# An encoder-decoder layer on one core: five small moves between ScalarE, VectorE and GpSimd

## The chip, the cores and the metric

The kernel runs on one core of a Trainium2 chip. A core has a matrix engine (TensorE, PE in the profile, its weight loads PEld), a vector engine (VectorE, DVE), a scalar engine (ScalarE, ACT), GpSimd (POOL) and SyncE (SP), which issues all transfers of this kernel. Each engine takes its own instructions in order; semaphores order the engines against one another. Results of TensorE go to PSUM, which has eight banks, and are read from there by VectorE or ScalarE.

The metric is the time of one execution on the device in microseconds (us). Before the change three runs took 3012.80, 3021.18 and 3019.86 us; the median is 3019.86.

## What is computed

One encoder layer on a short text (2 batches, 77 rows of width 512) and one decoder layer on a long sequence (2 batches, 2048 rows), all in fp32. 16 heads of width 32, an inner width of 2048. Cut to what matters:

```python
# encoder on ctx (77 rows): attention with relative bias, then relu feed-forward -> memory
yn = _ln(y, dec_n1_s, dec_n1_b)
y = y + _mha(yn, yn, dec_sa_in_w, ..., sb)        # causal self attention, 2048 x 2048, relative bias
y = y + _mha(_ln(y, dec_n2_s, dec_n2_b), memory, dec_ca_in_w, ..., cb)   # cross attention, 77 keys
h = _ln(y, dec_n3_s, dec_n3_b)
y = y + (relu(h @ dec_ff1_w.T + dec_ff1_b) @ dec_ff2_w.T + dec_ff2_b)

# _mha: scores = q k^T / sqrt(32) + bias; softmax over the keys; times v; out projection
# _ln:  (x - mean) * rsqrt(var + 1e-6) * s + b
```

The relative bias is the same for all keys further back than 127, so only the last two tiles of 128 keys of a row tile have a bias of their own.

## The kernel before, in words

The order of all instructions is written out by hand; nothing is scheduled by a tool.

**Self attention** takes up the time to about 1860 us. The sequence is cut into blocks of 512 rows (m = 0 to 3 per batch b) and these into 4 row tiles of 128 (t). Heads go in 4 groups of 4 (g). A unit is one (b, m, g, t): 128 rows against the keys up to and with their own tile, m*4 + t + 1 tiles of 128. These are cut into pieces of up to 4 tiles (`pieces`), and pieces go in pairs.

- `scores` (L344 on): for a piece, four matmuls, one for each head, on 32 rows of TensorE each, into four PSUM banks. In fp32 each is issued as two passes. VectorE then takes each bank to SBUF with its row maximum (L370), or, for the last two tiles, adds the bias (L377) and makes the negated maximum (L384). The exp is ScalarE's (L387); for m of 1 and more it is kept back and issued later by `exps`.
- `turn` (L397 on): for a pair of pieces, TensorE transposes the probabilities, 128 x 128 at a time (L411), up to four into one bank, which makes a load. A load is copied to SBUF by VectorE (L415) or by ScalarE (L417). Line 414 decides which. For m of 1 and more a load is one tile of keys for the four heads; a pair of two full pieces has 8 loads.
- `values` (L422 on): the turned pieces times v (L428), into a bank of their own.

Banks are given out in turn by `bank()`, 7 of them in self attention, so an eighth request waits for the release of the first. The main loop at the end of the kernel goes through the pairs: turn the pair; if the unit ends with it, run the jobs of the next slot (projections for later blocks, out projections, norms, and at first stages of the encoder); then scores of later pieces as far as memory allows, exps between them; then values of the pair.

**First cross attention.** In slots of the second batch's first blocks (about 966 to 1320 us) `first_cross` does the cross attention of the very first block.

**Cross attention and feed-forward**, from about 1862 us. For each of the 8 blocks (x) the feed-forward goes in 56 slots: 28 for the first product, 28 for the second, each by Strassen's scheme with seven products (`PARTS`, taken in the orders `ORDER`) in four quarters. `prepare` makes operands that are sums three slots ahead: on GpSimd, or on VectorE for `h` (L1114). `first_product` (L1125 on) adds a product into one or two quarters of hT; where it is the first to write a quarter it copies instead (L1142 or L1144, ScalarE), else VectorE adds (L1146); after the last, ScalarE adds the bias and takes the relu (L1149). The bank ring has four banks for products and four for all else.

Beside these slots runs the cross attention of the next block (`cross`, a plan with a list of stages for each slot, issued ahead of the slot's product). `norm_stages` has three stages: statistics (L726 to L729), centering on VectorE and the row of biases added on GpSimd (L735, L736), and the turned tile (transposes L741, then scale and bias by four activations, L744). For the norm before the cross attention these run at slots t, t + 2 and t + 4. `attend_stages` for row tile t starts at slot 14 + 7t: scores (L765, VectorE L772 to L775), exp (L778) two slots later, `normalize` three slots later (sums L783, reciprocals L784, product L785), `turned` at 6 (transposes L791, copies L793 and L795), times v at 9 (L802, L806), out projection at 11 (L811, L812). For the first block of a batch the tiles t of 0 and 1 need a bias, loaded by four DMAs into the tile of probabilities before the scores (`bias`, L103).

The lines that decide where things run, before:

```python
if o % 2 if first else o < 3 * len(loads) // 8:      # L414, turn: VectorE's loads
nc.scalar.activation(dst[:, c, :], pt[:, ts(c, P)], AF.Identity, bias=bi, scale=sc)   # L744
(engine or nc.gpsimd).tensor_tensor(prh, prh, ri[:, :, None].to_broadcast([P, H, S]), ALU.mult)  # L785
nc.scalar.copy(dst, got)                             # L1144
plan[at - 1 if t else at - 4].append(lambda t=t: bias(t))
```

Of the kernel before, what the change touches and what calls it, by code (L numbers as in the profile page):

```python
# [11 lines left out]
AF = mybir.ActivationFunctionType  # L12
ALU = mybir.AluOpType
# [4 lines left out]
P = 128  # L18
B, T, S, D = 2, 2048, 77, 512
H, HD, DFF = 16, 32, 2048  # L20
# [34 lines left out]
def tile_encoder_decoder(ctx: ExitStack, tc: tile.TileContext, ins, out):  # L55
    nc = tc.nc
# [92 lines left out]
    with (  # L149
# [245 lines left out]
        got = {}  # L395

        def turn(pieces):  # L397

            first = units[pieces[0][0]][1] == 0
            loads = []  # L400
            for n, k0, kn in pieces:
                ks = range(k0, k0 + kn)
                if first:
                    loads += [[(n, k, r) for k in ks] for r in range(HC)]
                else:
                    loads += [[(n, k, r) for r in range(HC)] for k in ks]
            for o, load in enumerate(loads):
                pt = bank()
                pts = in_turn("pts", pts_all).rearrange("p (x q) -> p x q", q=P)
                for x, (n, k, r) in enumerate(load):  # L410
                    nc.tensor.transpose(pt[:, ts(x, P)], state[n]["p"][r][:, ts(k, P)], ident)  # L411
                    got[n, k, r] = pts[:, x, :]
                w = len(load) * P
                if o % 2 if first else o < 3 * len(loads) // 8:  # L414
                    nc.vector.tensor_copy(pts[:, : len(load), :], pt[:, :w])  # L415
                else:
                    nc.scalar.copy(pts[:, : len(load), :], pt[:, :w])  # L417
                if first and o == len(loads) - 1:
                    exps(1)
            exps(1)  # L420
# [297 lines left out]
        def norm_stages(y, n, row, place, done):  # L718

            keep = {}  # L720

            def stats():
                st = sm.tile([P, 6], F32, name="bnst", tag="bnst")
                mv = sm.tile([P, 2], F32, name="cmv", tag="cmv", bufs=4)
                rs = sm.tile([P, 2], F32, name="crs", tag="crs", bufs=4)
                nc.vector.bn_stats(st, y())  # L726
                nc.vector.bn_aggr(mv, st)
                nc.vector.tensor_scalar_add(rs[:, 0:1], mv[:, 1:2], EPS)
                nc.gpsimd.tensor_tensor(rs[:, 1:2], rs[:, 0:1], mhalf[:, 0:1], ALU.pow)  # L729
                keep.update(mv=mv, rs=rs)  # L730

            def center():
                xn = keep["xn"] = place()
                mv, rs = keep["mv"], keep["rs"]
                nc.vector.tensor_scalar(xn, y(), mv[:, 0:1], rs[:, 1:2], ALU.subtract, ALU.mult)  # L735
                nc.gpsimd.tensor_tensor(y(), y(), row, ALU.add)  # L736

            def turned():
                xn, pt, dst = keep["xn"], bank(), done()
                for c in range(NC):  # L740
                    nc.tensor.transpose(pt[:, ts(c, P)], xn[:, ts(c, P)], ident)  # L741
                for c in range(NC):
                    sc, bi = vec(f"dec_{n}_s", c), vec(f"dec_{n}_b", c)
                    nc.scalar.activation(dst[:, c, :], pt[:, ts(c, P)], AF.Identity, bias=bi, scale=sc)  # L744

            return stats, center, turned

# [3 lines left out]
                nc.tensor.matmul(mm, w[:, c, :], nT[:, c, :], start=(c == 0), stop=(c == NC - 1))  # L751
            nc.vector.tensor_scalar(dst, mm, vec("dec_ca_in_b", o), SCALE, ALU.add, ALU.mult)

        def attend_stages(q, kTc, v, y, biased, pr, pts, place, w_o, engine=None):

            prh = pr.rearrange("p (h k) -> p h k", k=S)
            by_r = pr.rearrange("p (g r k) -> p g r k", r=HC, k=S)
            keep = {}

            def score():  # L760
                mx = sm.tile([P, NC, HC], F32, name="cmx", tag="cmx", bufs=3)
                banks = [bank() for _ in range(HC)]
                for g in range(NC):
                    for r in range(HC):
                        nc.tensor.matmul(  # L765
                            banks[r][:, ts(g, S)], q(g)[rows4(r)], kTc[rows4(r), g, :], start=True, stop=True
                        )
                for r in range(HC):
                    s = banks[r][:, : NC * S].rearrange("p (g k) -> p g k", k=S)
                    d = by_r[:, :, r, :]  # L770
                    if biased:
                        nc.vector.tensor_tensor(d, s, d, ALU.add)  # L772
                        s = d
                    nc.vector.tensor_reduce(mx[:, :, r], s, AX.X, ALU.max)
                    nc.vector.tensor_tensor(d, s, mx[:, :, r, None].to_broadcast([P, NC, S]), ALU.subtract)  # L775

            def exp():
                nc.scalar.activation(pr, pr, AF.Exp)  # L778

            def normalize():  # L780
                su = sm.tile([P, H], F32, name="csu", tag="csu", bufs=2)
                ri = sm.tile([P, H], F32, name="cri", tag="cri", bufs=2)
                nc.vector.tensor_reduce(su, prh, AX.X, ALU.add)  # L783
                nc.vector.reciprocal(ri, su)  # L784
                (engine or nc.gpsimd).tensor_tensor(prh, prh, ri[:, :, None].to_broadcast([P, H, S]), ALU.mult)  # L785

            def turned():
                for g in range(NC):
                    pt = bank()
                    for r in range(HC):  # L790
                        nc.tensor.transpose(pt[:S, ts(r, P)], prh[:, g * HC + r, :], ident)  # L791
                    if g % 2:
                        nc.vector.tensor_copy(pts(g), pt[:S, :])  # L793
                    else:
                        nc.scalar.copy(pts(g), pt[:S, :])  # L795

            def times_v():
                ot = bank()
                for g in range(NC):
                    for r in range(HC):  # L800
                        h = g * HC + r
                        nc.tensor.matmul(  # L802
                            ot[rows4(r), ts(g, P)], v[:, ts(h, HD)], pts(g)[:, ts(r, P)], start=True, stop=True
                        )
                keep["oT"] = place()
                nc.scalar.copy(keep["oT"], ot)  # L806

            def out():
                mm, oT = bank(), keep["oT"]
                for c in range(NC):  # L810
                    nc.tensor.matmul(mm, oT[:, ts(c, P)], w_o[:, c, :], start=(c == 0), stop=(c == NC - 1))  # L811
                nc.vector.tensor_tensor(y(), mm, y(), ALU.add)  # L812

            return score, exp, normalize, turned, times_v, out
# [78 lines left out]
        for x, (b, m) in enumerate(blocks):  # L893
            u = x * NU
            first = m == 0
# [24 lines left out]
            for g in range(NC):  # L920
# [3 lines left out]
                at = u + g * TB - 3  # L924
# [200 lines left out]
        def first_product(s):  # L1125
            x, layer, i, n = slots[s]
            a, b = operands[s]
            mm = ff_bank()
            for f in range(2):
                for c in range(2):  # L1130
                    nc.tensor.matmul(  # L1131
                        mm[:, ts(f, TOK)], a[:, c, ts(f, P)], b[:, c, :], start=(c == 0), stop=(c == 1)
                    )
            order = order_of(x, 1)
            got = mm.rearrange("p (f n) -> p f n", f=2)
            for sign, r, c in PARTS[i][2]:
                users = [j for j in order if (r, c) in [u[1:] for u in PARTS[j][2]]]
                f = (r - 1) * (NF // 2) + 2 * n
                dst = hT[:, f : f + 2, ts(c - 1, TOK)]
                if i == users[0]:  # L1140
                    if sign == "-":
                        nc.scalar.activation(dst, got, AF.Identity, scale=-1.0)  # L1142
                    else:
                        nc.scalar.copy(dst, got)  # L1144
                else:
                    nc.vector.tensor_tensor(dst, dst, got, SIGN[sign])  # L1146
                if i == users[-1]:
                    for e in range(2):
                        nc.scalar.activation(dst[:, e, :], dst[:, e, :], AF.Relu, bias=vec("dec_ff1_b", f + e))  # L1149
# [41 lines left out]
        def cross(x):  # L1191
# [9 lines left out]
            def bias(t):  # L1201
                bias_tile(pr.rearrange("p (h k) -> p h k", k=S), 2, P, S, 255 - P * t)
# [9 lines left out]
            for t in range(TB):  # L1212
                at = 14 + 7 * t
                y = lambda t=t: y_of(x, t)
                biased = m == 0 and t < 2
                if biased:
                    plan[at - 1 if t else at - 4].append(lambda t=t: bias(t))
                fs = attend_stages(
                    lambda g, t=t: qT[g // 2][:, g % 2, ts(t, P)], kTcs[b], vcs[b], y, biased, pr,
                    lambda g: pts_all[:S, g, :], place("xr"), wbt,  # L1220
                    None if t else nc.vector,
                )
                for k, f in zip((0, 2, 3, 6, 9, 11), fs):
                    plan[at + k].append(f)
# [133 lines left out]
```

## Time and profile before

| what | value |
|---|---|
| median of three runs | 3019.86 us |
| profiled execution, its own time | 3012.80 us |
| its span | 3011.0 us |
| TensorE busy | 2952.2 us, 98% of the span |
| VectorE busy | 2032.6 us, 68% |
| ScalarE busy | 1381.3 us, 46% |
| GpSimd busy | 733.6 us, 24% |
| mean TensorE clock granted | 0.99 |

The profile is one execution. The profiled execution's own time is its span and 1.8 us around it. Busy time of TensorE is that of pipelined matmuls, so 98% does not say that it runs at its peak; the chain of work that ended last and the waits tell where it is held. A group's row gives its line, engine, operation, tiles (out<-in) and shape, the count, then the busy time and the mean length of one in ns, then the idle time of the engine just ahead of it and what ended most of that. A row of the list of waits gives total us, number of waits and the longest. In the timeline a line is one instruction, or several of the same kind in a row, with start and length in us. An instruction's length has a tail that the next one on its engine overlaps: VectorE's copy of 128 x 512 from PSUM is 0.68 us long, but three in a row take 1.88 us.

### The profile page before, as it was taken

The page shows a single profiled execution, that of the slowest core. Times are in us where ns is not written, and L with a number is a line of the kernel's source. Part 1 is how long each engine was busy: PE and PEld are TensorE (multiplying, and loading weights), DVE is VectorE, ACT ScalarE, POOL GpSimd, SP SyncE. Part 2 cuts the span into 40 slices and gives each one's busy share as a digit, 9 for nine tenths or more (in the row PEclk, how much of TensorE's full clock was granted, in tenths as well). Part 3 has the DMA queues.
Part 4 walks back from the last instruction along what each step waited for, and adds up shares of the span by engine and source line. Part 5 has one row for each costly group of instructions (what it writes and reads, how often), then busy time and mean ns, then how long its engine had stood idle before and what let it go on. Part 6 is the DMA issues. An engine that isn't in the chain of part 4 may idle for free.

```text
span 3011.0 us, 60727 instructions
## 1 busy us (share of the span) xinstructions
PE 2952.2 (98%) x24440; PEld 2095.8 (70%) x24440; DVE 2032.6 (68%) x5806; ACT 1381.3 (46%) x2583; POOL 733.6 (24%) x594
## 2 busy tenths in 40 slices
PE   8899999999999999999999999999999999999999
PEld 5567666666677556666666677787878687878788
DVE  4766567767886777767867776666666666565645
ACT  3344456656666455556656666323232323232321
POOL 0100000000000101000000002464646464646465
PEclk9899999999999999999999999999999999999999
DMA  6413301200012411201200013200001000000000
GB/s 175 95 48 113 93 15 47 64 19 26 33 40 72 112 47 54 78 26 47 65 19 17 29 61 101 102 29 1 29 1 37 9 29 1 29 1 29 1 15 15
DMA packets 117645, 137.11 MB, mean 46 GB/s; under 512 B 18241, under 2 KB 73073, under 8 KB 117235
## 3 DMA queue, kind: packets, MB, share of 16 engines
q1 hardware_dynamic: 117362, 133.22, 15.3%
q8 instruction: 192, 3.15, 0.4%
q14 instruction: 91, 0.74, 0.1%
HBM read 111.33 MB, written 21.86 MB: 44 GB/s over the span
## 4 chain that ended last, share of the span: by engine, by line
PE 85%; DVE 12%; ACT 1%; issue 1%; DMA 1%; SPq 0%; POOL 0%; ACTq 0%; DVEq 0%; POOLq 0%
PE psum L1160 13%; PE psum L411 12%; PE psum L361 12%; PE psum L1131 10%; PE psum L428 7%; DVE pp L370 5%; PE psum L230 4%; PE psum L811 4%; PE psum L242 4%; PE psum L206 4%; PE psum L751 4%; PE psum L217 3%; DVE pp L377 2%; PE psum L791 2%; PE psum L765 1%; PE psum L802 1%
## 5 line engine op out<-in xcount | busy, mean ns | idle before, releaser
L387 ACT ACTIVATE pp<-pp,nm 128x128 f32<-128x128 f32 (+15 forms) x512 | 615.0, 1210 | 569.2 <-DVE nm L384 560.7
L370 DVE TENSOR_SCALAR_CACHE_REDUCE pp<-psum 128x512 f32<-128x512 f32 (+3 forms) x1024 | 555.0, 590 | 116.6 <-PE psum L361 114.8
L411 PE MATMUL psum<-ident,pp 128*128 128x128 f32 x4352 | 530.6, 277 | 7.1 <-DVE mx L377 2.9
L411 PEld LDWEIGHTS psum<-ident,pp 128*128 128x128 f32 x4352 | 475.3, 142 | 56.2 <-issue 27.9
L1114 POOL TENSOR_TENSOR vv<-pp 128x512 f32<-128x512 f32 x320 | 427.1, 1351 | 170.4 <-PE psum L1131 147.8
L361 PE MATMUL psum<-kT,q 32*128 32x512 f32 (+3 forms) x2560 | 442.8, 571 | 13.3 <-DVE pp L370 4.7
L417 ACT COPY pts<-psum 128x512 f32<-128x512 f32 (+2 forms) x744 | 373.0, 584 | 167.3 <-PE psum L411 79.0
L361 PEld LDWEIGHTS psum<-kT,q 32*128 32x128 f32 x2560 | 195.4, 185 | 238.7 <-issue 101.6
L428 PEld LDWEIGHTS psum<-pts,vv 128*32 128x32 f32 x8704 | 230.0, 111 | 115.1 <-issue 108.6
L428 PE MATMUL psum<-pts,vv 128*32 128x128 f32 x8704 | 285.4, 279 | 1.6 <-ACT pts L417 1.3
L415 DVE COPY pts<-psum 128x512 f32<-128x512 f32 (+2 forms) x392 | 237.2, 650 | 29.8 <-PE psum L411 29.6
L276 POOL TENSOR_TENSOR rstd<-rstd,mhalf 128x1 f32<-128x1 f32 x32 | 18.2, 570 | 973.7 <-DVE rstd L275 914.2
L1146 DVE TENSOR_TENSOR kT<-kT,psum 128x512 f32<-128x512 f32 x256 | 166.7, 681 | 114.0 <-PE psum L1131 108.1
L377 DVE CUSTOM_DVE_ANT_0 pp<-psum,bias 128x256 f32<-128x256 f32 (+1 forms) x512 | 209.6, 409 | 23.6 <-PE psum L361 15.7
L1149 ACT ACTIVATE kT<-kT,vecs 128x256 f32<-128x256 f32 x256 | 115.1, 499 | 191.2 <-DVE kT L1146 191.2
L1160 PE MATMUL psum<-vv 128*128 128x256 f32 x768 | 176.9, 381 | 0.0
L1131 PE MATMUL psum<-oT,vv 128*128 128x256 f32 x736 | 166.5, 380 | 0.0
L1144 ACT COPY kT<-psum 128x512 f32<-128x512 f32 x124 | 69.6, 588 | 204.0 <-DVE kT L1146 135.4
L1160 PEld LDWEIGHTS psum<-vv 128*128 128x128 f32 x768 | 143.1, 190 | 26.8 <-issue 9.5
L1131 PEld LDWEIGHTS psum<-oT,vv 128*128 128x128 f32 x736 | 138.8, 190 | 24.4 <-issue 6.2
L1114 DVE TENSOR_TENSOR vv<-kT 128x512 f32<-128x512 f32 x160 | 135.2, 860 | 13.1 <-PE psum L1160 12.1
L257 POOL TENSOR_TENSOR xr<-xr,row_dec_sa_out_b 128x512 f32<-128x512 f32 x30 | 38.1, 1273 | 398.6 <-DMA xr<-in_x_dram 320.2
(175 smaller groups left out, 3955.5 us busy)
## 6 DMA issues: line engine op xcount, KB each, us to landing
wqk<-in_dec_sa_in_wT_dram SPq DMA_DIRECT2D x64, 256.0 KB, 3.7
bias<-tz SPq DMA_DIRECT2D x128, 128.0 KB, 3.9
wbig<-in_dec_sa_in_wT_dram SPq DMA_DIRECT2D x8, 1024.0 KB, 8.0
vv<-in_enc_ff_wT_dram SPq DMA_DIRECT2D x8, 1024.0 KB, 5.4
wbig<-in_dec_sa_out_wT_dram SPq DMA_DIRECT2D x8, 1024.0 KB, 8.1
vv<-y SPq DMA_DIRECT2D x32, 256.0 KB, 3.3
out_dram<-vv SPq DMA_DIRECT2D x32, 256.0 KB, 2.0
xt<-in_x_dram SPq DMA_DIRECT2D x30, 256.0 KB, 3.8
```

The costliest lines, as they stand in the source:

```text
L361: nc.tensor.matmul(banks[r][:, : kn * P], q[rows4(r), ts(t, P)], kT[rows4(r), g, k0 * P : (k0 + kn) * P], start=True, stop=True,)
L370: nc.vector.tensor_scalar(p[:, k0 * P : (k0 + far) * P], s[:, : far * P], 1.0, None, ALU.mult, ALU.max, accum_out=st["mx"][:, r, c : c + 1],)
L377: nc.vector.tensor_tensor_reduce(p[:, (i + 1) * P - w : (i + 1) * P], s[:, far * P : kn * P], biases[b, m, g][:, r, 2 * P - w :], 1.0, LOW ...
L387: nc.scalar.activation(p, p, AF.Exp, bias=nm, accum_out=to)
L411: nc.tensor.transpose(pt[:, ts(x, P)], state[n]["p"][r][:, ts(k, P)], ident)
L415: nc.vector.tensor_copy(pts[:, : len(load), :], pt[:, :w])
L417: nc.scalar.copy(pts[:, : len(load), :], pt[:, :w])
L428: nc.tensor.matmul(ot[rows4(r), t, :], vv[:, k, ts(g * HC + r, HD)], got.pop((n, k, r)), start=(k == 0), stop=(k == i),)
L1114: engine.tensor_tensor(dst, quarter(*parts[0], n), quarter(*parts[2], n), SIGN[parts[1]])
L1131: nc.tensor.matmul(mm[:, ts(f, TOK)], a[:, c, ts(f, P)], b[:, c, :], start=(c == 0), stop=(c == 1))
L1146: nc.vector.tensor_tensor(dst, dst, got, SIGN[sign])
L1160: nc.tensor.matmul(mm[:, t, :], lhs[:, c, ts(t, P)], rhs[:, c, :], start=(n == 0 and c == 0), stop=(n == 3 and c == 1),)
```

## The change

It makes five edits, given here from the top of the diff.

1. In `turn`, for m of 1 and more, the first half of a pair's loads is copied by VectorE, in place of three eighths; the rest by ScalarE.
2. In `norm_stages`, of the four activations that finish a turned tile the two with even c become a `tensor_scalar` on VectorE.
3. In `attend_stages`, the product with the reciprocals is on GpSimd for every row tile. Before, `cross` put that of tile 0 on VectorE.
4. In `first_product`, where a product is the first to write a quarter with a plus and it is the second of the product's outputs, VectorE copies, not ScalarE.
5. In `cross`, the load of the second biased tile (t = 1) is listed in the slot of its scores, ahead of them, in place of the slot before.

```diff
@@ turn
-                if o % 2 if first else o < 3 * len(loads) // 8:
+                if o % 2 if first else o < len(loads) // 2:
                     nc.vector.tensor_copy(pts[:, : len(load), :], pt[:, :w])
                 else:
                     nc.scalar.copy(pts[:, : len(load), :], pt[:, :w])
@@ norm_stages, turned
-                    nc.scalar.activation(dst[:, c, :], pt[:, ts(c, P)], AF.Identity, bias=bi, scale=sc)
+                    if c % 2:
+                        nc.scalar.activation(dst[:, c, :], pt[:, ts(c, P)], AF.Identity, bias=bi, scale=sc)
+                    else:
+                        nc.vector.tensor_scalar(dst[:, c, :], pt[:, ts(c, P)], sc, bi, ALU.mult, ALU.add)
@@ attend_stages, normalize
-                (engine or nc.gpsimd).tensor_tensor(prh, prh, ri[:, :, None].to_broadcast([P, H, S]), ALU.mult)
+                nc.gpsimd.tensor_tensor(prh, prh, ri[:, :, None].to_broadcast([P, H, S]), ALU.mult)
@@ first_product
-            for sign, r, c in PARTS[i][2]:
+            for k, (sign, r, c) in enumerate(PARTS[i][2]):
...
                     if sign == "-":
                         nc.scalar.activation(dst, got, AF.Identity, scale=-1.0)
+                    elif k:
+                        nc.vector.tensor_copy(dst, got)
                     else:
                         nc.scalar.copy(dst, got)
@@ cross
                 if biased:
-                    plan[at - 1 if t else at - 4].append(lambda t=t: bias(t))
+                    plan[at if t else at - 4].append(lambda t=t: bias(t))
                 fs = attend_stages(
                     lambda g, t=t: qT[g // 2][:, g % 2, ts(t, P)], kTcs[b], vcs[b], y, biased, pr,
                     lambda g: pts_all[:S, g, :], place("xr"), wbt,
-                    None if t else nc.vector,
                 )
```

The words that go with the change also name the order of the scores of a pair and of the exps; the diff holds no edit of that order.

More of the change, by code (lines that the diff above doesn't have):

```diff
@@ L752, in q_group, with attend_stages @@
             nc.vector.tensor_scalar(dst, mm, vec("dec_ca_in_b", o), SCALE, ALU.add, ALU.mult)
-        def attend_stages(q, kTc, v, y, biased, pr, pts, place, w_o, engine=None):
+        def attend_stages(q, kTc, v, y, biased, pr, pts, place, w_o):
             prh = pr.rearrange("p (h k) -> p h k", k=S)
```

## The prediction

> **What bounds the kernel now.** I read the page from the engine totals down: the chain of work that ended last, the costliest groups, then the timeline of single spots.
>
> ```profile
> PE 2952.2 (98%) x24440; PEld 2095.8 (70%) x24440; DVE 2032.6 (68%) x5806; ACT 1381.3 (46%) x2583; POOL 733.6 (24%) x594
> ...
> PE 85%; DVE 12%; ACT 1%; issue 1%; DMA 1%; SPq 0%; POOL 0%; ACTq 0%; DVEq 0%; POOLq 0%
> ...
> L417 ACT COPY pts<-psum 128x512 f32<-128x512 f32 (+2 forms) x744 | 373.0, 584 | 167.3 <-PE psum L411 79.0
> L415 DVE COPY pts<-psum 128x512 f32<-128x512 f32 (+2 forms) x392 | 237.2, 650 | 29.8 <-PE psum L411 29.6
> ```
>
> TensorE holds 85% of the chain, VectorE (DVE) 12%, ScalarE (ACT) 1%. The change moves work from the engine with 1% of the chain to the one with 12%. Time read by stage (busy time in stretches of the span): in self attention of the two longest rows of blocks (415 to 966 us) VectorE is busy 412 of 551 us and TensorE 548; in the last stage (1862 to 3011) VectorE 705 of 1149, TensorE 1131. So VectorE has free time everywhere, and the question is whether it is free at the spots where TensorE waits for it. The list of waits says whom ScalarE itself waits for:
>
> ```profile
> ACT pp L387 <- DVE nm L384: 560.7, 126, 10.0
> ...
> PEld psum L361 <- DVE pp L370: 71.0, 154, 0.8
> ```
>
> The exps (L387) wait 561 us in all for maxima that VectorE makes. A ScalarE with less to copy gets to them earlier and waits longer.
>
> One spot, the turn of unit 54's first pair, in the timeline (start, length, engine and line, in brackets the idle time before and its releaser):
>
> ```profile
> 791.37 3.07 PEld L411 LDWEIGHTS psum<-ident,pp 128*128 128x128 f32 x28 [0.20 <-DVE mx L377]
> 793.57 2.59 ACT L417 COPY pts<-psum 128x512 f32<-128x512 f32 x5
> 794.09 1.89 DVE L415 COPY pts<-psum 128x512 f32<-128x512 f32 x3
> 795.43 3.03 PE L361 MATMUL psum<-kT,q 32*128 32x512 f32 x16
> 796.59 0.69 DVE L370 TENSOR_SCALAR_CACHE_REDUCE pp<-psum 128x512 f32<-128x512 f32 x1 [0.62 <-PE psum L361]
> 798.39 1.69 PEld L428 LDWEIGHTS psum<-pts,vv 128*32 128x32 f32 x64 [0.76 <-issue]
> ```
>
> VectorE copies loads 0 to 2, ScalarE 3 to 7. VectorE then idles 0.62 us until the next scores have ended. That gap is the cover for one copy more.
>
> **Edit 1, the turned pieces (L414).** For m of 1 and more VectorE takes half of a pair's loads, in place of three eighths rounded down. By the lengths of the pieces that is one copy more in 4, 7 and 8 turns per group of heads for m = 1, 2, 3; times 4 groups and 2 batches, 152 copies. Three copies take 1.89 us, the last with its tail, so a further one takes 0.61 (five on ScalarE take 2.59, 0.49 each). Added to VectorE: 152 x 0.61 = 93 us. Between 0 and 93 us of it can show; I take the spots one by one.
>
> Behind a turn that ends a unit come jobs on TensorE of 3.6 us and more (L242 x8, 3.70 in the timeline); VectorE's copy ends in that time, and a gap of 1.8 us is still left at 807.64. Nothing is charged. This covers every turn of m = 1 and about half of the others.
>
> Behind a unit's first pair (64 of them, m = 2 and 3) the scores follow at once. There are 7 banks in a ring, so the moved load's bank is the one that the third head of the next scores writes. At unit 54 it comes free at 795.97 + 0.61 = 796.58 in place of 794.1, and the third head, which could start just behind 795.43, starts at 796.6. A head has two pieces of two passes to make; a single piece of two passes takes 1.11 us from its start to the values behind it (unit 32, 424.12 to 425.23), so four take about 2.1: 796.6 + 2.1 = 798.7, against 798.39. Cost 0.3 us. VectorE's next evacuation still starts at 796.59, so nothing piles up. Going through the timeline for all 64: 20 such turns have VectorE that late (14 at 0.3, 6 at 0.5 where the second piece is shorter) = 7.2 us; 8 turns of seven loads with one piece behind, 6 at 0.13 and 2 at 0.5 = 1.8; 4 turns where values follow at once and the fourth load's copy is late by 0.4 = 1.6; in the other 32 the third head's bank is free in time. Sum +10.6 us. Ends: 0 (all hidden), and 31 if a third of the 93 shows.
>
> [...]
>
> **Edit 2, normed rows turned (L744).** 64 calls, of which two of four activations go to VectorE: 128 instructions. The nearest row is L301, the same operation on VectorE: 402 ns, four in 1.37, so 0.34 each; on ScalarE four take 1.51. **Edit 4, first products (L1144).** By the order of products, the second output's first use is a plus in 3 of 7 products for seven blocks, 2 for the first: (7x3 + 2) x 4 = 92 of 124 copies, at 0.61 each (L415). Together +44 and +56 us of VectorE, of which the chain of the first eight product slots matters. There VectorE is dense (start, length):
>
> ```profile
> 2028.54 0.69 DVE L726 BATCH_NORM_STATS2 bnst<-vv 128x6 f32<-128x512 f32 x1 [2.17 <-DMA vv<-y]
> ...
> 2032.54 1.41 DVE L735 TENSOR_SCALAR pts<-vv,cmv,crs 128x512 f32<-128x512 f32 x1
> ...
> 2035.73 0.60 PE L741 MATMUL psum<-ident,pts 128*128 128x128 f32 x4
> ```
>
> The fourth row tile's centering ends at 2033.95, and its transposes run at 2035.73: 1.8 us of slack. Put in its queue ahead of it and behind the load that lands at 2028.54: three copies (1.83) and two pairs of turned columns (1.36), 3.2 in all. It is late by 1.4 us if the centering keeps its 1.41, by 0.5 if it takes the 0.54 of its fastest rows. I take 0.9, for the six blocks with a full cross attention beside them: +5.4 us. Ends: 0, and 1.4 + 0.7 more for the projections that follow, 13 us. In the other slots VectorE idles 1 to 2.7 us at a time (L752, L1146), so 0. In the early cross attention (966 to 1320 us) the 16 instructions of edit 2 have ScalarE's other two beside them: 0, give or take 2.
>
> **Edit 3, the first tile's normalizing (L785).** It goes from VectorE to POOL.
>
> ```profile
> 2072.17 2.33 DVE L785 TENSOR_TENSOR oT<-oT,cri 128x1232 f32<-128x1232 f32 x1
> 2074.65 1.94 PE L791 MATMUL psum<-ident,oT 128*77 128x128 f32 x16 [0.89 <-DVE oT L785]
> 2078.34 1.04 ACT L795 COPY pts<-psum 77x512 f32<-77x512 f32 x2
> 2078.96 1.28 PE L765 MATMUL psum<-pts,bias 32*128 32x77 f32 x24 [0.64 <-ACT pts L795]
> ```
>
> On POOL it takes 2.25 us (median of 21), so the wait of 0.89 stays. VectorE, 2.3 us freer, evacuates six products earlier; ScalarE's copies hang on these, and the second wait, 0.64, goes: six blocks, -3.9 us. Queued behind it on POOL is the operand of slot 20 (L1114, 1.27 us): 2074.5 + 1.3 = 2075.8, used about 2076.4, so just in time. Ends: -6, and +8 if that operand is late by 1.3 six times. The biased block, where VectorE took 1.44, pays 0.8 us more: +0.9.
>
> [...]
>
> **Edit 5, the second biased tile's loads.** It is named one slot later. The queue that issues it (SP) holds nothing between the two places, and its four DMAs wait for the transposes before (issued at 2372.52, transposes from 2370.50) either way: 0; at worst one slot, 2 us, once.
>
> **Sum.** 10.6 + 5.4 - 3.9 + 0.9 = +13 us. The profiled execution took 3012.8 us (3011.0 of span and 1.8 around it): 3025.8 by its own time. It was the fastest of three; the median is 3019.86, 7.1 above, so I name 3033, 0.43% slower. About 0.3%, 9 us, is what a measurement of this kernel tells from no change.
>
> **The rivals.** (a) All hidden: the third heads' banks come in time because the passes interleave otherwise than I think, and the first slots' centering runs at 0.54. For it: VectorE is busy 75% at most. Against: TensorE already waits 71 us for VectorE's evacuations (L361 by L370). About 0, 3016 to 3024. (b) VectorE becomes the bound: its busy time grows by 93 + 44 + 56 - 16 = 177 us to some 2210; each late turn starts the next one late. For it: the chain already runs through L370 and L377. Against: the gaps of 0.6 to 1.8 us that reset it. A third of 93 plus 9: +40, 3060. (c) Faster: ScalarE is what scores and values wait for. Its price is the weight loads' waits on ScalarE's copies and exps, 7.4 + 4.2 + 2.9 us, less the little that stays: -12, 3008. It decides if ScalarE's copies end over 0.6 us behind VectorE's at most turns; at unit 54 they end at 796.16 and 795.97. Against: the 561 us above. (d) The words for the change speak of the order of scores and exps; the diff leaves that order as it is, so nothing is counted for it.
>
> **How the numbers follow.** Forecast 0.50 (+4 to +24 alone), (a) 0.22, (b) 0.18, (c) 0.10. Slower by over 9 us: 0.36 of the forecast's 0.50, and (b): 0.54. Faster: (c) and 0.02 of (a): 0.12. Within: 0.34. The range runs from 3013 to 3058: it leaves out most of (c) and the upper part of (b), about 2 in 10.
>
> **What would show it.** VectorE's copies at L415 x544, ScalarE's at L417 x592, each of the two busy totals moved (about +177 and -176 us: 152 x 0.49, 92 x 0.59 and 128 x 0.38 off ScalarE). At unit 54, scores that last about 3.3 us in place of 2.96 with the third head waiting for VectorE's fourth copy; 0.5 to 1.4 us of wait at L741's last transposes of a block; no wait of L765 behind L795. I am wrong if TensorE's waits on L415 stay at 11.6 us (weight loads of L361), or if L370's gap of 0.62 us turns into a queue that grows from turn to turn.

## The result and the profile after

The kernel after takes 3034.76 us (median of four runs, 3029.29 to 3036.24), the kernel before beside it 3020.52. The ratio is 1.0048, 95% interval 1.0027 to 1.0070: 14.2 us slower, where the forecast had +13 and 3033. Most of the interval lies beyond the 0.3% that the prediction named. The profiled execution after took 3036.24 us with a span of 3034.5. Against the profiled execution before (3012.80, 3011.0) that is 23.5 us more in span; part of that is the clock granted to TensorE, 0.987 against 0.990, which comes up again below.

The page of after, engine totals, chain and the two groups of copies of turned pieces:

```profile
PE 2967.9 (98%) x24440; PEld 2102.0 (69%) x24440; DVE 2205.1 (73%) x6171; ACT 1229.2 (41%) x2211; POOL 737.5 (24%) x601
...
PE 82%; DVE 12%; issue 2%; POOL 2%; DMA 1%; ACT 1%; SPq 0%; POOLq 0%; DVEq 0%; ACTq 0%
...
L417 ACT COPY pts<-psum 128x512 f32<-128x512 f32 (+3 forms) x592 | 300.1, 576 | 234.5 <-PE psum L411 192.5
L415 DVE COPY pts<-psum 128x512 f32<-128x512 f32 (+2 forms) x544 | 329.4, 659 | 30.3 <-PE psum L411 28.6
```

The counts are the forecast's, 544 and 592. VectorE is busy 173 us longer (177 predicted), ScalarE 152 less (176 predicted). VectorE's share of the chain is 12% as before: it has taken 173 us more and has not become what the end hangs on. In the chain POOL now has 2% (0% before) and issue 2% (1%).

The list of waits of after (total us, number, longest); behind the edits the lines of the kernel lie 1 to 5 further down, so that before's L744 is now L745 (ScalarE) and L747 (VectorE), and L785, L791 and L765 are L788, L794 and L768:

```profile
ACT pp L387 <- DVE nm L384: 563.6, 125, 10.1
...
PEld psum L361 <- DVE pp L370: 64.8, 126, 0.8
...
PEld psum L361 <- DVE pts L415: 26.7, 104, 0.3
...
DVE vv L747 <- ACT vv L745: 15.3, 28, 1.0
```

Three things are to be seen. The exps on ScalarE wait for maxima as long as before (563.6 us), so the relief of ScalarE bought nothing there. TensorE's weight loads wait 26.7 us for VectorE's copies at L415, in place of 11.6. And there are waits that before had not: VectorE and ScalarE wait for each other (L747 and L745), and TensorE's transposes wait for ScalarE's columns (L741, 3.7 us over 6 waits).

**A turn in self attention.** Unit 54's first pair again, in the timeline of after:

```profile
797.92 2.48 DVE L415 COPY pts<-psum 128x512 f32<-128x512 f32 x4
...
799.27 3.18 PE L361 MATMUL psum<-kT,q 32*128 32x512 f32 x16
...
800.42 0.69 DVE L370 TENSOR_SCALAR_CACHE_REDUCE pp<-psum 128x512 f32<-128x512 f32 x1
800.46 1.16 PEld L361 LDWEIGHTS psum<-kT,q 32*128 32x128 f32 x12 [0.30 <-DVE pts L415]
...
802.38 0.70 PEld L428 LDWEIGHTS psum<-pts,vv 128*32 128x32 f32 x28 [0.76 <-issue]
```

The fourth copy ends at 800.40, and the third head's weights go in at 800.46, as the forecast had it. From the scores' start at 799.27 to the values at 802.38 it is 3.11 us, against 2.96 before. So this turn costs 0.15 us, not 0.3.

**The first slots of a feed-forward block.** The timeline of after, a tile's turned columns and the centering behind them:

```profile
2043.72 0.40 DVE L747 TENSOR_SCALAR vv<-psum,vecs 128x128 f32<-128x128 f32 x1
2044.16 0.46 ACT L745 ACTIVATE vv<-psum,vecs 128x128 f32<-128x128 f32 x1 [2.72 <-DVE vv L747]
2044.65 0.41 DVE L747 TENSOR_SCALAR vv<-psum,vecs 128x128 f32<-128x128 f32 x1 [0.53 <-ACT vv L745]
2044.98 0.54 DVE L735 TENSOR_SCALAR xt<-vv,cmv,crs 128x512 f32<-128x512 f32 x1
2045.10 0.46 ACT L745 ACTIVATE vv<-psum,vecs 128x128 f32<-128x128 f32 x1 [0.48 <-DVE vv L747]
...
2045.58 0.66 PE L741 MATMUL psum<-ident,xt 128*128 128x128 f32 x4 [0.42 <-DVE xt L735]
...
2048.57 0.63 PE L741 MATMUL psum<-ident,pts 128*128 128x128 f32 x4 [0.61 <-ACT vv L745]
```

The four turned columns lie in one PSUM bank. Even columns are VectorE's, odd ones ScalarE's, and each instruction starts when the other engine's has ended: 2043.72, 2044.16, 2044.65, 2045.10. VectorE is held from 2043.72 to 2044.98, 1.26 us for a work of 0.7 (two columns in a row take 0.72 in e24_halves, below). The centering (L735) comes behind that in its queue, and TensorE waits for both.

**The first tile's normalizing**, now on POOL:

```profile
2085.56 2.25 POOL L788 TENSOR_TENSOR oT<-oT,cri 128x1232 f32<-128x1232 f32 x1 [3.99 <-DVE cri L787]
...
2087.86 1.97 PE L794 MATMUL psum<-ident,oT 128*77 128x128 f32 x16 [0.82 <-POOL oT L788]
...
2091.49 1.13 PE L768 MATMUL psum<-pts,bias 32*128 32x77 f32 x32
```

From the start of the transposes to the next scores it is 3.63 us, before 4.31 (2074.65 to 2078.96): the wait of 0.64 is gone. The 32 matmuls of the scores themselves take 1.13 us; before they took 1.60, because a second wait for ScalarE's copies lay between them.

Setting TensorE's instructions of the two traces side by side one by one, and taking out what stretches of half clock cost (the last section has these), I counted by how much after falls back at each place: 6 to 7 us at first pairs and single pieces of self attention, 1.7 in the first cross attention, 1.9 at the first slots of four of the six blocks, 2.9 at those of the biased block and 4.0 at those of the last, and 1.1 to 1.2 gained at the first tile's normalizing in each of five. Of the last block's 4.0, 2.1 is a wait of VectorE for a DMA, at 2792.00, that the run of edits 2 and 4 alone (e24, below) doesn't have at this place: all its waits of that kind make 1.2 us. "By the count" below means such a comparison with before.

### The profile page after: what moved, and what is told of

It is laid out like the page before. It is cut to its first block, busy times and chain, and to the rows that moved or that the text cites. A ratio compares the mean times of both kernels' runs of the same rounds, so it can differ in the third digit from the quotient of the medians.

```text
span 3034.5 us, 60596 instructions
## 1 busy us (share of the span) xinstructions
PE 2967.9 (98%) x24440; PEld 2102.0 (69%) x24440; DVE 2205.1 (73%) x6171; ACT 1229.2 (41%) x2211; POOL 737.5 (24%) x601
## 4 chain that ended last, share of the span: by engine, by line
PE 82%; DVE 12%; issue 2%; POOL 2%; DMA 1%; ACT 1%; SPq 0%; POOLq 0%; DVEq 0%; ACTq 0%
PE psum L1165 13%; PE psum L411 12%; PE psum L361 12%; PE psum L1134 8%; PE psum L428 7%; DVE pp L370 4%; PE psum L230 4%; PE psum L814 4%; PE psum L754 4%; PE psum L206 4%; PE psum L242 4%; PE psum L217 3%; DVE pp L377 2%; PE psum L794 2%; DVE pts L415 1%
## 5 line engine op out<-in xcount | busy, mean ns | idle before, releaser
L387 ACT ACTIVATE pp<-pp,nm 128x128 f32<-128x128 f32 (+15 forms) x512 | 613.9, 1205 | 572.2 <-DVE nm L384 563.6
L370 DVE TENSOR_SCALAR_CACHE_REDUCE pp<-psum 128x512 f32<-128x512 f32 (+3 forms) x1024 | 555.4, 590 | 78.7 <-PE psum L361 75.2
L411 PE MATMUL psum<-ident,pp 128*128 128x128 f32 x4352 | 530.1, 277 | 7.5 <-DVE mx L377 2.9
L411 PEld LDWEIGHTS psum<-ident,pp 128*128 128x128 f32 x4352 | 473.8, 142 | 58.1 <-issue 24.4
L361 PE MATMUL psum<-kT,q 32*128 32x512 f32 (+3 forms) x2560 | 449.7, 571 | 12.6 <-DVE pp L370 4.7
L1117 POOL TENSOR_TENSOR vv<-pp 128x512 f32<-128x512 f32 x320 | 415.5, 1315 | 145.8 <-PE psum L1134 125.6
L417 ACT COPY pts<-psum 128x512 f32<-128x512 f32 (+3 forms) x592 | 300.1, 576 | 234.5 <-PE psum L411 192.5
L361 PEld LDWEIGHTS psum<-kT,q 32*128 32x128 f32 x2560 | 201.5, 185 | 238.2 <-issue 95.5
L415 DVE COPY pts<-psum 128x512 f32<-128x512 f32 (+2 forms) x544 | 329.4, 659 | 30.3 <-PE psum L411 28.6
L206 PE MATMUL psum<-nT,wqk 128*128 128x512 f32 x256 | 119.2, 610 | 0.3
```

The costliest lines, as they stand in the source:

```text
L206: nc.tensor.matmul(mm, w[:, c, :], nTs[b, m][:, c, :], start=(c == 0), stop=(c == NC - 1))
L361: nc.tensor.matmul(banks[r][:, : kn * P], q[rows4(r), ts(t, P)], kT[rows4(r), g, k0 * P : (k0 + kn) * P], start=True, stop=True,)
L370: nc.vector.tensor_scalar(p[:, k0 * P : (k0 + far) * P], s[:, : far * P], 1.0, None, ALU.mult, ALU.max, accum_out=st["mx"][:, r, c : c + 1],)
L387: nc.scalar.activation(p, p, AF.Exp, bias=nm, accum_out=to)
L1117: engine.tensor_tensor(dst, quarter(*parts[0], n), quarter(*parts[2], n), SIGN[parts[1]])
```

## The experiments

All twelve start from the kernel before. The theory: three separate things make up the result, namely the third head's bank in self attention (edit 1), the alternation of two engines on one bank at the start of a block (edits 2 and 4), and a saving at the first tile's normalizing (edit 3). The rival for the first two: it is VectorE's load as such, and each microsecond that is put on it costs its share wherever it is put.

**How the clock was taken out.** Each run has its mean granted clock recorded beside it, and the runs of one kernel spread by some 12 us along it. In the 33 runs of before made beside the last four kernels, the nine at a clock of 0.986 took 3022.6 us on average, the eight at 0.987 3020.9, the four at 0.988 3017.8, the eleven at 0.989 3014.7: about 2.6 us for 0.001. I fitted one straight line to the runs of a kernel and those of before beside it, with one slope for both and an offset for the kernel. The offset is the column "at equal clock", with its 95% interval. This was chosen after the runs had been seen, and a kernel may itself change the clock; what a change costs its user is the ratio.

| kernel | ratio to before, 95% interval | that is, us | mean clock less before's, thousandths | at equal clock, us |
|---|---|---|---|---|
| e1_only | 1.0016 [1.0007, 1.0025] | +4.8 | -0.3 | +4.7 ± 0.8 |
| e1_last | 1.0004 [0.9995, 1.0013] | +1.2 | -0.7 | -0.1 ± 1.0 |
| e1_more | 1.0109 [1.0096, 1.0122] | +33 | -0.6 | +30.3 ± 2.0 |
| e1_swap | 1.0004 [0.9994, 1.0013] | +1.2 | -2.6 | -5.8 ± 1.2 |
| e2_only | 1.0020 [1.0007, 1.0033] | +6.0 | -1.2 | +2.7 ± 1.4 |
| e4_only | 1.0006 [0.9996, 1.0016] | +1.8 | -0.2 | +0.4 ± 1.2 |
| e24 | 1.0053 [1.0039, 1.0066] | +16.0 | -0.8 | +13.7 ± 1.3 |
| e24_halves | 1.0023 [1.0012, 1.0034] | +6.9 | -0.5 | +4.4 ± 1.2 |
| e3_only | 0.9990 [0.9982, 0.9999] | -3.0 | -1.1 | -5.9 ± 0.9 |
| e3_unbiased | 0.9985 [0.9976, 0.9994] | -4.5 | -0.6 | -5.7 ± 0.9 |
| e5_only | 1.0000 [0.9990, 1.0010] | 0 | -0.4 | -0.4 ± 0.9 |
| best | 0.9986 [0.9976, 0.9997] | -4.2 | -3.1 | -11.9 ± 1.2 |

### Edit 1: the load or the bank

`e1_only` is edit 1 alone.

```diff
-                if o % 2 if first else o < 3 * len(loads) // 8:
+                if o % 2 if first else o < len(loads) // 2:
```

> Edit 1 alone: VectorE copies half of a pair's loads. Bank theory (the third head's scores wait for the bank of VectorE's last copy, at a unit's first pair only): +7 us (+5 to +9), in steps of 0.15 to 0.6 us at the first pairs of m = 2 and 3, and nothing at m = 1. Load theory (VectorE's added time shows in one share wherever it lies): 93 of the 177 us added, so 93/177 of the 14 us measured, +7.5 us, spread over m = 1, 2 and 3.

`e1_last` gives VectorE the same number of copies, but the additional one is the pair's last load, whose bank is not the third head's.

```diff
+                if o % 2 if first else o < 3 * len(loads) // 8 or (o == len(loads) - 1 and len(loads) // 2 > 3 * len(loads) // 8):
```

> As edit 1 alone, 152 copies more for VectorE, but the one more is a pair's last load in place of the next one. Bank theory: the third head's bank is ScalarE's again and free early, so +1 us (-1 to +3). Load theory: the same added time on VectorE, +7.5 us.

Edit 1 alone costs 4.8 us, and the same copies on the last load 1.2, with an interval that holds zero; at equal clock 4.7 and -0.1. The ratios' intervals overlap (2.1 to 7.5 us and -1.5 to 3.9); at equal clock they are apart. The waits for L415 are those of after with the one, the same 26.7 us over 104 waits, and nearly those of before with the other. First before, then e1_last:

```profile
PEld psum L361 <- DVE pts L415: 11.6, 51, 0.3
```

```profile
PEld psum L361 <- DVE pts L415: 12.0, 53, 0.3
```

By the count the turns of m of 2 and 3 lose 6 us with e1_only, and nothing with e1_last. So 93 us more on VectorE (152 x 0.61) cost nothing that can be measured when the bank that comes late is not the next one wanted. It is the bank, not the load. The 15 us by which the wait grows are not what it costs: other waits of the same weight loads shrink beside it, in after those for L370 from 71.0 to 64.8 us and those on issue from 101.6 to 95.5.

`e1_more` gives VectorE five eighths, 264 copies more than before, one beyond edit 1 in a pair of eight loads.

```diff
+                if o % 2 if first else o < 5 * len(loads) // 8:
```

> VectorE takes five eighths of a pair's loads: 264 copies more than before, where edit 1 has 152. Bank and cover theory: at a first pair with full pieces VectorE's fifth copy ends 0.6 us after the next scores, so the cover of 0.62 us is gone and its evacuations start late: about 0.6 us at each of some 32 late first pairs on top of edit 1, +20 us or more. Load theory: 264/152 of the 4.8 us measured for edit 1, +8.

It costs 33 us. At unit 54 the fourth copy ended just as the next maximum could start (800.40, 800.42); a fifth has no gap left to go into. By the count the 18 first pairs that cost 0.15 us each with edit 1 cost 0.74 here, and 14 others, free with edit 1, cost about 0.3. Up to the gap a copy is nearly free; beyond it the next one costs 0.59 of its 0.61 us. This is what rival (b) expects of VectorE, one step further on than the change goes, but for one thing: the turns between, which end a unit, add nothing, so no turn hands its delay on to the next.

### Edits 2 and 4: what holds VectorE at the start of a block

`e24` is both edits, `e2_only` and `e4_only` one each, as in the change.

> Edits 2 and 4 alone (turned norms and first products). Queue theory (VectorE held in the first eight product slots, where it alternates with ScalarE on one bank): +13 us (+10 to +16), of it 1.9 per block at the transposes of the norm ahead of the cross attention, for six blocks, and 1.9 once in the first cross attention. Load theory: 100 of 177 us added, +8 us. What the prediction reckoned: +5.4.

> Edit 2 alone: the two even columns of a turned tile on VectorE, so that VectorE and ScalarE take turns on one bank. Alternation theory: each call holds VectorE for 1.26 us (0.40, a wait of 0.53 for ScalarE, 0.41), two of them stand ahead of the fourth centering, 2.5 us against 1.8 of slack: +0.7 us a block for six blocks and +1.6 in the first cross attention, +6 us. If VectorE were held only for its own 0.68 us a call: 1.4 us, inside the slack, 0 a block, and 0 to +1 in all.

> Edit 4 alone: 92 first copies on VectorE. Three of them (1.8 us) stand ahead of the fourth centering, against 1.8 us of slack; each also waits for ScalarE's copy out of the same bank. Queue theory: +0.3 us a block, +2 us (0 to +4). Load theory: 56 of the 100 us that edits 2 and 4 add, so 56% of the 16 us measured for both, +9.

`e24_halves` is e24 with the same work for each engine, but VectorE takes columns 0 and 1, ScalarE 2 and 3.

```diff
-                    if c % 2:
+                    if c >= 2:
                         nc.scalar.activation(dst[:, c, :], pt[:, ts(c, P)], AF.Identity, bias=bi, scale=sc)
```

> Edits 2 and 4, but in a turned tile VectorE takes the first two columns and ScalarE the last two, so that the engines change over once. VectorE's work is the same as with edits 2 and 4. Alternation theory: VectorE is held for 0.68 us a call in place of 1.26, two calls ahead of the fourth centering, so 1.2 of the 2.1 us a block come back: +8 us (+5 to +11) in place of +16. Load theory: no change, +16.

e24, e4_only and e24_halves came out as the theory of one bank had it, not as the rival. e2_only did not: its 6.0 is the number named, but at equal clock it is 2.7, and by the count it costs 0.0 to 0.15 us at the first slots of five of the six blocks, where 0.7 was expected of each, 1.9 in the biased block and 1.6 in the first cross attention. So the alternation alone fits into the slack of most blocks.

Together the two edits cost 16.0 us, in halves 6.9; the intervals are apart, and the counts of instructions are equal. The sum of the two alone is 7.8, half of what they cost together. The groups of L741 show why. In before these two rows have 0.0 us of idle time in them. In e24 (the last column is TensorE's idle time ahead of them, and what ended it):

```profile
L741 PE MATMUL psum<-ident,xt 128*128 128x128 f32 x152 | 23.1, 275 | 4.6 <-ACT vv L745 2.5 <-DVE xt L735 2.1
...
L741 PE MATMUL psum<-ident,pts 128*128 128x128 f32 x72 | 11.0, 275 | 3.3 <-DVE pts L735 2.1 <-ACT vv L745 1.2
```

In e24_halves:

```profile
L741 PE MATMUL psum<-ident,xt 128*128 128x128 f32 x152 | 23.1, 275 | 0.2
...
L741 PE MATMUL psum<-ident,pts 128*128 128x128 f32 x72 | 11.0, 275 | 0.0
```

7.9 us of waits, against 0.2; edit 4 alone has 0.1, and after 9.5. Edit 2 alone has 1.0, nearly all in one row:

```profile
L741 PE MATMUL psum<-ident,pts 128*128 128x128 f32 x72 | 10.9, 273 | 0.9 <-DVE pts L735 0.9
```

The timeline at the same spot, first e24, then e24_halves:

```profile
2043.47 0.40 DVE L747 TENSOR_SCALAR vv<-psum,vecs 128x128 f32<-128x128 f32 x1
2043.91 0.46 ACT L745 ACTIVATE vv<-psum,vecs 128x128 f32<-128x128 f32 x1 [1.51 <-DVE vv L747]
2044.41 0.41 DVE L747 TENSOR_SCALAR vv<-psum,vecs 128x128 f32<-128x128 f32 x1 [0.53 <-ACT vv L745]
2044.73 0.54 DVE L735 TENSOR_SCALAR pts<-vv,cmv,crs 128x512 f32<-128x512 f32 x1
```

```profile
2043.44 0.72 DVE L747 TENSOR_SCALAR vv<-psum,vecs 128x128 f32<-128x128 f32 x2
2044.08 0.53 DVE L735 TENSOR_SCALAR pts<-vv,cmv,crs 128x512 f32<-128x512 f32 x1
2044.25 0.81 ACT L745 ACTIVATE vv<-psum,vecs 128x128 f32<-128x128 f32 x2 [1.48 <-DVE vv L747]
```

VectorE is held 0.64 us by its two columns in a row, 1.26 in turns with ScalarE. In these slots the alternation is what costs, together with the first copies of edit 4 in the same queue. The fourth centering takes 1.41 us in before and 0.54 in e24 and 0.53 in e24_halves (rows above), so by my estimate the slack of 1.8 us grows to some 2.7. Two calls with alternate columns (2.52 us) fit in and three first copies (1.83) fit in; both together (4.35) are 1.7 late. The first copies themselves wait for ScalarE's copy of the same product 12.7 us in all (e4_only, 92 copies). By the count e24 loses 1.8 to 2.2 in five blocks and 3.0 in the biased one. The 4.4 to 6.9 us that e24_halves still costs lie, by the count, at the same slots with 0.6 to 1.0 us a block, and in the first cross attention with 1.7, as much as e24 loses there. So in that stretch the alternation is not what costs; what does was not traced. A split over two banks was not tried.

In these rows and those of after no column starts before the other engine's has ended. Here the waiting cost 0.62 us of VectorE a call (1.26 less 0.64).

### Edit 3: the first tile's product

`e3_only` is edit 3 alone, `e3_unbiased` leaves the first tile of the one biased block on VectorE.

```diff
-                    None if t else nc.vector,
+                    nc.vector if biased and not t else None,
```

> Edit 3 alone: the first tile's product with the reciprocals on GpSimd. Queue theory: the scores behind it no longer wait for ScalarE's copies, -1.1 us a block for six blocks, less 0.9 once at the biased block, -5.5 us (-7 to -4). Load theory: 16 us less on VectorE, -1.3 us. Prediction's bad case (GpSimd's next operand late): +8.

> The third edit alone, but in the five blocks without a bias; in the biased block the first tile's rows stay on VectorE. If the saving is 1.1 us in each of the five blocks, as the alignment of the third edit's run had it, and the biased block's loss came from POOL's late product there: -5.5 us (-7 to -4). If the biased block lost nothing by it: -3 us, as with the third edit in all six.

They save 3.0 and 4.5 us, and at equal clock 5.9 and 5.7: five blocks at 1.1 us, and the biased block neither wins nor loses measurably. The 3.0 lies just outside what I had expected of e3_only (-7 to -4), at equal clock inside. Both values named for e3_unbiased, -5.5 and -3, lie within its interval of -7.2 to -1.8, so the ratio alone doesn't decide between them. I had put down a loss of 2 us and more in the biased block to POOL, from the traces of after and of e3_only. A window over its transposes shows another cause. The columns are the stretch, its length, busy time of PE, PEld, VectorE, ScalarE and GpSimd, then the granted clock (PEclk), and last the share and rate of DMA. First e3_only, then e3_unbiased:

```profile
2373.80:2377.20 3.40, 3.40 (x16) 3.27 (x15) 1.83 (x3) 1.88 (x4) 3.40 (x4) 0.52 0.00 0
```

```profile
2370.20:2373.60 3.40, 3.37 (x24) 3.14 (x24) 3.40 (x6) 2.26 (x6) 0.00 (x0) 1.00 0.07 8
```

The granted clock is 0.52 in the one and 1.00 in the other, and the sixteen transposes (L791) take 3.31 us and 1.94. A half clock does not need this product on POOL: before, which has it on VectorE, shows 0.50 from 2386.81 on for 3.41 us, with POOL idle throughout; that begins while TensorE waits 2.54 us for ScalarE (L811 behind L806). What brings it on at the transposes of e3_only was not shown. Apart from the clock, POOL's part is the wait of 3.21 us ahead of the transposes in e3_only against 2.36 in before: 0.85, the forecast's 0.9. By the count the scores behind them win 1.06 back.

### Edit 5

`e5_only` is edit 5 alone.

```diff
-                    plan[at - 1 if t else at - 4].append(lambda t=t: bias(t))
+                    plan[at if t else at - 4].append(lambda t=t: bias(t))
```

> The fifth edit alone: the issue of a tile's bias one slot later. The forecast has it at nothing: 0 (-1 to +1). If the issue's place counted, the tiles 1 to 3 of the one biased block would each be late by the slot's 2 to 3 us: +6 or more.

Nothing, as expected: the interval is -3 to +3 us, and the +6 lies outside it.

### The other way round, and a better version

`e1_swap` leaves VectorE three eighths, but the last ones. `best` is that and e3_unbiased.

```diff
-                if o % 2 if first else o < 3 * len(loads) // 8:
+                if o % 2 if first else o >= len(loads) - 3 * len(loads) // 8:
```

> The kernel before with the same three eighths of a pair's loads copied by VectorE, but the last three in place of the first three; ScalarE takes the first five. The counts stay (392 copies on VectorE in self attention). Theory of what is late: in a pair's first loads VectorE is still in the rows of the previous scores, so the first loads' banks come free late (0.39 us at unit 54's eighth load, 0.18 and 0.30 us at its scores), while ScalarE has been done half a microsecond longer; with ScalarE on the first loads TensorE should wait less: -3 to -8 us, and the wait of TensorE's weight loads at L361 on L415 should shrink. Rival: who copies the last loads is what the scores and VectorE's next row of scores wait for, and a VectorE copy takes 0.61 us: +2 to +8 us.

> The two last kernels' edits together: VectorE copies the last three of eight loads, and the first tile's rows leave VectorE in the five blocks without a bias. They lie in different stretches, so the sum of the two: about -9 us if both theories hold (-14 to -6), -3 to +3 if the swap of the loads costs what its rival says.

By the ratio the swap brings nothing, and neither theory's range holds +1.2. At equal clock it is -5.8, which the first theory had. Both are true: the mean clock of its runs was 0.984 to 0.987, before's 0.986 to 0.990.

At unit 54 the expected gain is there: the pair's 32 transposes run in one row, without the pause of 0.39 us for L415 that before has at 794.83, and by the count the turn gains 0.3. But it does not stand for the rest. By the count the turns of m of 2 and 3 lose 3.6 us in sum: the transposes (L411) win 8.1 and the scores behind them (L361) lose 10.5, as the rival had it. The gain lies at m = 1, 4.5 us in the first batch and 5.4 in the second, at the jobs behind the turn that ends a unit. An example is the transposes of a norm (L294), in before and in e1_swap:

```profile
282.05 0.65 PE L294 MATMUL psum<-ident,xt 128*128 128x128 f32 x4 [1.14 <-DVE pts L415]
```

```profile
279.53 0.60 PE L294 MATMUL psum<-ident,xt 128*128 128x128 f32 x4
```

In before VectorE has the turn's first two loads, and comes to them only at 281.31, behind its rows of the scores and the statistics of a norm; TensorE waits for their banks. With ScalarE on the first loads it does not wait. So the first theory holds where a unit ends with the turn, and the rival where the scores follow at once. A swap at m = 1 alone was not tried.

The waits of L361's weight loads say little of this: 17.9 us for ScalarE's copies and 2.9 for VectorE's, where before has 7.4 and 11.6. `best` is 4.2 us faster than before (0.9 to 7.2), faster than the kernels before and after; by the ratio it is no better than e3_unbiased alone (4.5). The two edits add up at equal clock (-5.8 and -5.7 against -11.9); the clock takes about 8 us of that back. Why TensorE is granted less with the swap was not found.

## Why the prediction was right

The size was right: +13 predicted, +14.2 measured (8 to 21). At equal clock the parts, measured alone, make 4.7 + 13.7 - 5.9 - 0.4 = +12.1. But that the sum is so near is luck: at equal clock edit 1 was put 6 us too high and edits 2 and 4 8 too low, and edit 3 saved 3 more than was reckoned.

| step | predicted, us | alone, at equal clock | by the ratio |
|---|---|---|---|
| edit 1 | +10.6 | +4.7 | +4.8 |
| edits 2 and 4 | +5.4 | +13.7 | +16.0 |
| edit 3, biased block included | -3.9 + 0.9 | -5.9 | -3.0 |
| edit 5 | 0 | -0.4 | 0 |

- **Edit 1.** The mechanism is shown: the fourth copy's bank, the third head waits for it, and 152 copies elsewhere cost nothing that can be measured (e1_last). The mis-sized term is the time behind the third head's start. I took 2.1 us for two heads from a single piece at unit 32; from 800.46 to 802.38 it is 1.92. That makes 0.15 a turn in place of 0.3. By the count the 20 late turns cost 2.8 us where I had 7.2, the turns of seven loads 2.4 (1.8) and those with values at once 1.5 (1.6): 6.7 in all, within the ratio's interval of 2.1 to 7.5.
- **Edits 2 and 4.** The place was right, the first slots' centering, and so was the slack, 1.8 us with the centering at 1.41 and some 2.7 with it at 0.54. The step that was mis-sized is "two pairs of turned columns (1.36)". I priced them at 0.68 a pair by VectorE alone, from L301, and overlooked that the other two columns of the bank go to ScalarE in between. At 1.26 a pair the same sum is 1.83 + 2.52 = 4.35, 1.2 more than my 3.2. With the centering at the 0.54 that it showed, 0.5 + 1.2 = 1.7 us a block are late, where e24 has 1.8 to 2.2 by the count, and 3.0 in the biased block. In the first cross attention, priced at 0 give or take 2, edit 2 costs 1.6 by the count.
- **Edit 3.** The wait of 0.64 went and the 0.89 stayed (0.82), as said. The term is too small because only the wait ahead of the scores was in it: the second of ScalarE's copies also held the scores' own row, 1.60 us against 1.13. 0.68 + 0.47 = 1.15 a block, the 1.1 to 1.2 counted. The biased block paid its 0.9 and won that back at its scores. POOL's operands for the next slots came in time, as said: the list of waits of e3_unbiased has no product of L1131 waiting for POOL, that of e3_only 0.2 us once.
- **Edit 5** cost nothing, as said.
- **The rivals.** All hidden (a) falls with the waits at L741 and L415. VectorE as the bound (b) falls for this change by its 12% of the chain and by e1_last; e1_more shows that its price begins with one copy more, though not a queue that grows from turn to turn. Faster (c) falls: the exps wait 563.6 us as before. The words for the change (d) were rightly not counted: the diff moves neither scores nor exps.

That L415's waits would grow was the test I had set. They did, by 15 us, three times the cost.

## What to carry to other kernels

Before work is moved to an engine with free time, look at which buffer each moved instruction releases and who wants that next: the same 152 copies cost 4.8 us on the fourth load and nothing measurable on the last. Where two engines read one PSUM bank in turns, try a contiguous half for each: here the same work cost 16 us by alternate columns and 6.9 by halves. And add up slack for all edits that use the same queue at the same spot, since two edits of 6.0 and 1.8 us made 16 together.

## What was unexpected about the hardware

- **The granted clock comes in steps.** Its records in before and after hold stretches at 0.5 of 3.41 us or two, three or four times that, but for the last in each, at or just behind the end of the span (1.58 and 4.46). The profiled execution before has 12 of these stretches with 63 us in all, after 14 with 80. By my estimate one such 3.4 us takes 0.00057 off the mean clock (half of 3.41 in 3011) and costs up to 1.7 us, 3.0 for 0.001, near the 2.3 to 2.9 of the lines fitted to the runs of each kernel. Most of the spread between runs of before follows the clock: in the three sets of them beside the other kernels 82 to 88% of the variance lies on a straight line.
- In the feed-forward such stretches come behind a TensorE that is idle for over half of the 3.5 us ahead: it is busy 1.46 of them in before (stretch at 2386.81), 0.32, 1.25 and 1.47 in after (2386.89, 2403.96, 3032.01). In after the transposes of the biased block follow an idle time of 3.22 us and take 3.60, where those at 2087.86, shown above, take 1.97:

```profile
2386.94 3.60 PE L794 MATMUL psum<-ident,oT 128*77 128x128 f32 x16 [3.22 <-POOL oT L788]
```

- In self attention, though, stretches stand behind 17 us in which by my sum over the trace TensorE is busy throughout (at 676.74 and 1581.27 in before, at 567.59, 680.23, 1478.95 and 1591.59 in after); no run here shows why.
